# The second batch's products with x and with q in plain fp32, its q turned by TensorE, and the order written anew

## The chip, the core and the metric

The kernel runs on one core of one Trainium2 chip. A core has TensorE (PE, matrix products into PSUM), VectorE (DVE), ScalarE (ACT), GpSimd (POOL) and SyncE (SP, which here only issues DMAs). The metric is the device time of one execution in microseconds, given as the median of several runs. Each engine works through its own queue in order; a wait at the head of a queue holds everything behind it.

## The reference

The input x has 16 batches of 512 tokens with 256 features. Each batch goes through linear attention with 16 heads of 16 features, a residual and a layer norm, then a feed-forward layer with ternary weights, a residual and a layer norm:

```python
q, k, v = proj(Wq, bq), proj(Wk, bk), proj(Wv, bv)      # x @ W.T + b, per head
q_kern = exp(q - max(q));  k_kern = exp(k - max(k))      # max over the 16 features of a head
kv = einsum('bhsd,bhse->bhde', k_kern, v)
denom = einsum('bhqd,bhd->bhq', q_kern, sum_s(k_kern)) + 1e-06
y = einsum('bhqd,bhde->bhqe', q_kern, kv) / denom
x = layernorm(x + y @ Wo.T + bo)
Wq1, Wq2 = (clip(round(W / (mean(|W|) + 1e-5)), -1, 1) for W in (W1, W2))
x = layernorm(x + relu(x @ Wq1.T + b1) @ Wq2 + b2)
```

## The kernel before, in words

A batch is one tile of 128 partitions by 4 groups of tokens (t = 0 to 3) by 256 features. What TensorE does for a batch:

- `qk{t}` (L673 to L685): q and k of one group of tokens, 128x512, from xT and both weights. DVE adds the bias (`mxa`, L690) and takes the maximum (`mxb`, L696), POOL or DVE subtracts it (`mxs`, L700), ACT takes exp (`ex`, L711).
- `pks` (L758): the sum of exp(k) over all tokens, from a sum over the groups (`ks`, L734) that is split into two parts (`ksh`, `ksl`). DVE makes the denominators with it (`dena`, `denb`, `denc`), and `nrm{h}` (L790) divides exp(q) by them; the result is qs.
- `g{c}` (L813) or `gF{c}` (L809): the product of x with exp(k). The kernel uses that k_kern'v = (k_kern'x) Wv', so that v is never computed. `ge` (L832) copies the result, `kv` (L840) multiplies it with Wv, `kvm`, `kvp` mask it and add the bias' share, `m` (L868) multiplies with Wo.
- q turned: qs must have its features on the partitions.
- `o{h}` (L1066) or `oF{h}` (L1062): the product of the turned q with m. `or{t}` (L988) adds it to the residual, and the layer norm follows (`nm`, `nq`, `nv`, `np`, `na`: mean, squares, variance, pow on POOL, apply).
- x1 turned, then `f{f}` (L1098, 8 steps) and `z{f}` (L1135, 8 steps) for the feed-forward layer, with `ha`, `hc`, `hb` between them on ACT and DVE, and the second norm (`zr`, `ym` to `ya`), then the store.

Two ways to multiply are used. In plain fp32 one matmul takes the two fp32 operands. In the split way each operand is held as two rounded parts, high and low, and three products (high-high, high-low, low-high, `TERMS`) are summed. The split way needs the parts: a rounding copy on ACT and a subtraction on DVE or POOL for every operand: `xs`, `xsl0`, `xsl1` (L646, L652) for x, the second exp (L713) and `ek0`, `ek1` (L719) for exp(k), `me` and `ml` (L878, L883) for m, and `be`, `bl` (L928, L933) for the turned q.

Two ways to turn are used as well. TensorE turns 128x128 blocks against an identity (L941), and ACT copies the result out of PSUM; or a batch is "moved": DVE turns 32x32 blocks (`qtr`, L898), SP writes the tile to DRAM (`qtw`) and reads it back in four pieces that put the blocks in their places (`qtd`).

Constants say which batch does what: batches below FB, GB, OB take their products with the q/k weights, with x, and with q in plain fp32, and MOVED names the batches whose q (`qt`) and x1 (`xt1`) are moved:

```python
FB = 1
GB = 1
OB = 1
MOVED = {"qt": range(1, 16), "xt1": range(1, 15)}
        if b in MOVED[key]:
            moved()
            return
        for c in range(EC):
            one(c)
                if b < GB:
                    nc.tensor.matmul(s.pg[:, c, :], s.x32[:, t, cc], s.ex[:, t, E:2 * E],
                                     start=(t == 0), stop=(t == T - 1))
```

The order of all work is written out by hand: `ORDER` (from L109) gives each step of each batch a number, the steps are emitted by it, and each engine runs its instructions in the order in which they were emitted. `OTHER` (from L51) names the batches for which a step that two engines could do goes to the second of the two. Start-up steps stand in the same order: `lqk`, `wh`, `wl` load and split the q/k weights, `lw`, `sa`, `sr`, `tot`, `half`, `qn`, `qz` load the feed-forward weights and make them ternary, `warm` are matmuls without a use. The tile xt32 (the turned x from DRAM, `ldt0`, `ldt1`, L612) has two buffers, x32 (`ldx`, L640) has four. In PSUM, the `qk` products and all turns share two banks, `o`, `g`, `kv`, `m` and `pks` share two, `f` has two and `z` two.

Of the kernel before, what the change touches and what calls it, by code (L numbers as in the profile page):

```python
# [43 lines left out]
GB = 1  # L44
OB = 1
KB = 0
JB = 2
MOVED = {"qt": range(1, 16), "xt1": range(1, 15)}
# [3 lines left out]
    "xtl1": (1, 3, 7, 15),  # L52
    "qn2": (0,),
    "ks": (0, 1, 2, 4, 5, 8, 11),
    "ksl": (0, 1, 2, 3, 4, 5, 7, 8, 10, 11, 12, 13, 14, 15),
    "qn0": (0,),
    "xsl1": (1, 3, 12, 13),
    "qn1": (0,),
    "qn3": (0,),
    "mxs0": (1, 9, 10, 11, 12, 13, 14),  # L60
    "qn6": (0,),
    "nm0": (0, 1, 2, 3, 5, 7, 8, 9, 10, 11, 14),
    "ek0": (1, 3, 4, 8, 9, 10, 11, 12, 13, 14),
    "ek1": (1, 2, 3, 4, 6, 7, 8, 9, 11, 12, 13, 14, 15),
    "nv0": (0, 3, 8, 9, 13),
    "kvp": (1, 3, 4, 5, 7, 9, 12, 14, 15),
    "xb0": (1, 3, 7, 12, 15),
    "kvl": (1, 2, 3, 4, 5, 7, 8, 10, 11, 12, 13, 15),
    "xsl0": (2, 4),
    "xb1": (1, 3, 4, 13),  # L70
    "qn7": (0,),
    "qn4": (0,),
    "x1b1": (0, 6, 11),
    "qn5": (0,),
    "qtbl0": (2, 3, 4, 9, 15),
    "x1b0": (0, 1, 7, 9, 11, 12, 13),
    "xt1bl0": (1, 2, 3, 5, 7, 10, 14),
    "hc4": (1, 5, 6, 9, 14),
    "nrm0": (3, 7, 8, 9, 10, 11),
    "na0": (2, 6, 8, 14),  # L80
    "mxs1": (4, 7, 13, 14),
    "mxs2": (4, 7, 13, 14, 15),
    "xt1bl1": (2, 3, 4, 5, 6, 10, 12),
    "ym0": (1, 2, 5, 8),
    "na2": (3, 4, 15),
    "hc5": (2, 7, 13, 14, 15),
    "hc7": (2, 5, 10, 11, 12, 13, 15),
    "qtbl1": (4, 7, 15),
    "yv0": (2, 3, 4, 6, 11),
    "nrm1": (5, 11, 13, 14),  # L90
    "ya0": (2, 6, 7, 8, 12, 13, 15),
    "na1": (4, 7, 11, 14, 15),
    "mxs3": (7, 10, 13),
    "hc2": (4, 5, 6, 8, 11, 13, 14),
    "hc3": (4, 12, 13, 14),
    "ya3": (3, 6, 11, 12, 13),
    "hc6": (4, 8, 9),
    "xtl0": (10, 13),
    "hc1": (5, 7, 10, 11, 12, 15),
    "ya2": (4, 11, 13, 14, 15),  # L100
    "ya1": (5, 7, 11, 12, 13, 14),
    "hc0": (9, 10, 13, 14),
    "na3": (10, 13),
    "ym2": (15,),
    "yv1": (15,),
    "yv2": (15,),
    "ym3": (15,),
# [5 lines left out]
    "wh0": (3,),  # L113
    "ldt0a": (4, 0, 0, 0, 0, 0, 0, 0, 0, 0, 0, 0, 0, 0, 0, 0),
    "qkF0_0": (5, 0, 0, 0, 0, 0, 0, 0, 0, 0, 0, 0, 0, 0, 0, 0),
    "wl0": (6,),
    "ldt1a": (7, 0, 0, 0, 0, 0, 0, 0, 0, 0, 0, 0, 0, 0, 0, 0),
    "wh1": (8,),
    "wl1": (9,),
    "lbqk": (10,),  # L120
    "qkF0_1": (11, 0, 0, 0, 0, 0, 0, 0, 0, 0, 0, 0, 0, 0, 0, 0),
    "mxa0": (12, 101, 119, 271, 362, 547, 589, 741, 927, 1135, 1172, 1344, 1546, 1661, 1766, 1938),
    "ldt0": (0, 13, 61, 158, 231, 346, 335, 545, 743, 893, 792, 1025, 1049, 1380, 1562, 1505),
    "xt0": (0, 14, 62, 177, 257, 386, 387, 643, 809, 894, 831, 1113, 1220, 1402, 1644, 1808),
    "mxb0": (15, 113, 120, 279, 365, 550, 598, 744, 932, 1169, 1173, 1345, 1547, 1662, 1783, 1976),
    "ldt1": (0, 16, 72, 108, 208, 221, 411, 416, 690, 915, 826, 1099, 1082, 1363, 1631, 1725),
    "xt1": (0, 17, 77, 117, 239, 344, 467, 630, 775, 916, 901, 1231, 1218, 1392, 1657, 1847),
    "xtl1": (0, 18, 94, 141, 248, 402, 516, 634, 817, 933, 1024, 1249, 1219, 1393, 1705, 1848),
    "qkF1_0": (19, 0, 0, 0, 0, 0, 0, 0, 0, 0, 0, 0, 0, 0, 0, 0),
    "ldt1b": (20, 0, 0, 0, 0, 0, 0, 0, 0, 0, 0, 0, 0, 0, 0, 0),  # L130
    "mxs0": (21, 115, 155, 306, 420, 551, 662, 784, 961, 1170, 1326, 1401, 1548, 1672, 1826, 2008),
    "exF0": (22, 0, 0, 0, 0, 0, 0, 0, 0, 0, 0, 0, 0, 0, 0, 0),
    "ldt0b": (23, 0, 0, 0, 0, 0, 0, 0, 0, 0, 0, 0, 0, 0, 0, 0),
    "xtl0": (0, 24, 69, 183, 278, 413, 521, 659, 816, 945, 975, 1296, 1351, 1403, 1666, 1814),
    "qkF1_1": (25, 0, 0, 0, 0, 0, 0, 0, 0, 0, 0, 0, 0, 0, 0, 0),
    "mxa1": (26, 88, 160, 232, 322, 474, 670, 765, 871, 1053, 1184, 1394, 1452, 1680, 1840, 1903),
    "mxb1": (27, 89, 164, 244, 323, 514, 712, 799, 889, 1067, 1281, 1408, 1453, 1681, 1841, 1914),
    "lw0": (28,),
    "sa0": (29,),
    "mxs1": (30, 114, 165, 280, 446, 515, 730, 840, 953, 1100, 1300, 1409, 1511, 1728, 1842, 1990),  # L140
    "exF1": (31, 0, 0, 0, 0, 0, 0, 0, 0, 0, 0, 0, 0, 0, 0, 0),
    "lvo": (32,),
    "woh": (33,),
    "qkF2_0": (34, 0, 0, 0, 0, 0, 0, 0, 0, 0, 0, 0, 0, 0, 0, 0),
    "qkF2_1": (35, 0, 0, 0, 0, 0, 0, 0, 0, 0, 0, 0, 0, 0, 0, 0),
    "mxa2": (36, 58, 162, 205, 444, 472, 625, 783, 973, 1045, 1294, 1333, 1561, 1599, 1732, 1942),
    "mxb2": (37, 59, 185, 302, 447, 541, 626, 791, 974, 1107, 1305, 1334, 1563, 1605, 1733, 2004),
    "ldx": (38, 70, 179, 154, 326, 524, 642, 845, 931, 1076, 1269, 1386, 1556, 1706, 1717, 1948),
# [223 lines left out]
def block_kernel(ctx: ExitStack, tc: tile.TileContext, x, xT, wqT, wkT, wvT, woT,  # L372
# [221 lines left out]
    def steps(b):  # L594
# [632 lines left out]
```

## Time and profile before

| | us |
|---|---|
| median of 3 runs | 484.31 (484.08 to 484.88) |
| the profiled execution's own time | 484.78 |
| its span on the core | 483.1 |
| TensorE busy / share | 469.2 / 97% |
| DVE busy / share | 439.9 / 91% |
| ACT busy / share | 406.2 / 84% |
| POOL busy / share | 378.8 / 78% |
| first `f` of batch 0 starts | 47.93 |
| last matmul starts | 476.94 |

In a row of the trace the columns are the start, the length, the engine, the line and operation, the tile written and the tiles read, the size and a count; in square brackets stands the engine's idle time before it and who ended it. Matmuls are pipelined: a record of TensorE is longer than the distance to the next one, so the cost of a matmul is read from start to start. A plain fp32 matmul shows as two records. The granted TensorE clock was 0.999 of full speed over the span.

### The profile page before, as it was taken

The numbers are of one execution on the slowest core, as the hardware profiler recorded it, in microseconds if no ns is written. First come the engines' busy times: TensorE is split into PE (matmuls) and PEld (weight loads), VectorE is DVE, ScalarE is ACT, GpSimd is POOL, SyncE is SP. The second block draws the span as 40 slices with busy tenths as digits, with TensorE's granted clock in tenths as the row PEclk, the third lists the DMA queues.
The fourth block names the chain that finished last, engine by engine and source line by source line (L and its number), as shares of the span: only waits on it lengthen the run. The fifth ranks groups of instructions, "written<-read, shape, count | busy, mean of one in ns | idle before, by whom it ended". The sixth has DMA issues, their size and how long they took to land.

```text
span 483.1 us, 9025 instructions
## 1 busy us (share of the span) xinstructions
PE 469.2 (97%) x2976; PEld 415.9 (86%) x2976; DVE 439.9 (91%) x859; ACT 406.2 (84%) x923; POOL 378.8 (78%) x391
## 2 busy tenths in 40 slices
PE   8989999999999999999999999999999999999995
PEld 5567899899888998989989898889989898898984
DVE  2889999999999999999999998999999988998964
ACT  3897998998889788997987989688898979966774
POOL 1788898976958999896989799798898778744524
PEclk9999999999999999999999999999999999999999
DMA  6931325071542745345332605323445145124102
GB/s 227 309 140 43 89 88 196 24 229 55 160 125 68 216 143 153 104 127 175 130 133 87 199 22 188 118 99 121 152 130 148 51 156 150 44 89 132 44 1 88
DMA packets 36671, 59.84 MB, mean 124 GB/s; under 512 B 4240, under 2 KB 22672, under 8 KB 36624
## 3 DMA queue, kind: packets, MB, share of 16 engines
q1 hardware_dynamic: 36048, 58.74, 38.1%
q8 instruction: 23, 0.38, 0.3%
q10 hardware_dynamic: 576, 0.52, 0.3%
q14 instruction: 24, 0.20, 0.2%
HBM read 35.66 MB, written 23.59 MB: 123 GB/s over the span
## 4 chain that ended last, share of the span: by engine, by line
PE 79%; DVE 6%; POOL 5%; DMA 4%; ACT 3%; issue 2%; ACTq 0%; POOLq 0%; DVEq 0%
PE ph L1098 22%; PE pz L1135 21%; PE pqk L680 14%; PE po L1066 8%; PE pg L813 8%; PE pkv L840 2%; PE pm L868 2%; DMA w32qk<-in_wkT_dram 1%; DMA x<-in_x_dram 1%; POOL qk L700 1%; DMA w<-in_w1T_dram 1%; DVE x1b L1037 1%; PE pg L809 1%; PE pks L758 1%; POOL rstd_z L1020 1%
## 5 line engine op out<-in xcount | busy, mean ns | idle before, releaser
L1104 ACT ACTIVATE ph<-ph,b_sb 128x512 f32<-128x512 f32 x128 | 83.7, 657 | 20.9 <-PE ph L1098 19.9
L700 POOL TENSOR_TENSOR qk<-qk,mx 128x512 f32<-128x512 f32 x45 | 51.6, 1150 | 12.7 <-DVE mx L696 12.1
L690 DVE TENSOR_TENSOR qk<-pqk,bqk 128x512 f32<-128x512 f32 x64 | 43.2, 679 | 3.8 <-PE pqk L680 1.5
L696 DVE TENSOR_REDUCE mx<-qk 128x32 f32<-128x512 f32 x64 | 43.4, 679 | 1.2
L711 ACT ACTIVATE ex<-qk 128x512 f32<-128x512 f32 x64 | 40.4, 631 | 3.9 <-POOL qk L700 3.1
L790 POOL TENSOR_TENSOR qs<-ex,rden 128x512 f32<-128x512 f32 x22 | 26.2, 1204 | 13.2 <-DVE rden L782 13.1
L1005 ACT ACTIVATE junk_z<-x1b,nm_z 128x256 f32<-128x256 f32 x64 | 32.2, 505 | 2.4 <-POOL nm_z L999 2.2
L1035 ACT ACTIVATE x<-x,nmr_o,rstd_o 128x256 f32<-128x256 f32 x50 | 28.0, 600 | 7.3 <-POOL nmr_o L1022 7.3
L1005 ACT ACTIVATE junk_o<-x,nm_o 128x256 f32<-128x256 f32 x64 | 32.1, 503 | 0.4
L823 POOL TENSOR_TENSOR x<-x,bo_bc 128x512 f32<-128x512 f32 x23 | 30.6, 1335 | 0.1
L1081 POOL TENSOR_TENSOR x1b<-x,b_bc 128x512 f32<-128x512 f32 x22 | 29.5, 1346 | 1.4 <-ACT x L1035 1.4
L988 DVE SCALAR_TENSOR_TENSOR x1b<-pz,x1b 128x256 f32<-128x256 f32 x64 | 24.7, 417 | 1.7 <-PE pz L1135 1.5
L988 DVE SCALAR_TENSOR_TENSOR x<-po,x 128x256 f32<-128x256 f32 x64 | 24.3, 417 | 1.5 <-PE po L1066 1.0
L1035 ACT ACTIVATE x1b<-x1b,nmr_z,rstd_z 128x256 f32<-128x256 f32 x39 | 21.8, 598 | 4.2 <-POOL nmr_z L1022 4.2
L777 DVE TENSOR_REDUCE den<-dent 128x64 f32<-128x1088 f32 x16 | 20.5, 1281 | 0.2
L762 DVE TENSOR_TENSOR dent<-ex,pks 128x1024 f32<-128x1024 f32 x16 | 19.4, 1214 | 1.0 <-PE pks L758 1.0
L898 DVE STREAM_TRANSPOSE rqT<-qs 128x1024 f32<-128x1024 f32 x15 | 18.6, 1240 | 1.7 <-POOL qs L790 1.3
L1020 POOL TENSOR_TENSOR rstd_z<-var_z,expo 128x4 f32<-128x4 f32 (+1 forms) x19 | 19.2, 1011 | 1.0
L898 DVE STREAM_TRANSPOSE rx1T<-x 128x1024 f32<-128x1024 f32 x14 | 17.4, 1240 | 1.9 <-ACT x L1035 1.2
L1020 POOL TENSOR_TENSOR rstd_o<-var_o,expo 128x4 f32<-128x4 f32 x16 | 18.1, 1131 | 0.8
L840 PEld LDWEIGHTS pkv<-g,wv 128*128 128x128 f32 x128 | 16.2, 191 | 2.2 <-ACT g L832 1.3
L840 PE MATMUL pkv<-g,wv 128*128 128x128 f32 x128 | 17.0, 276 | 0.7 <-ACT g L832 0.7
(899 smaller groups left out, 2122.6 us busy)
## 6 DMA issues: line engine op xcount, KB each, us to landing
x<-in_x_dram SPq DMA_DIRECT2D x16, 512.0 KB, 4.5
xt<-in_xT_dram SPq DMA_DIRECT2D x30, 256.0 KB, 4.1
wqT<-rqT SPq DMA_DIRECT2D x15, 512.0 KB, 2.6
dqT<-wqT SPq DMA_DIRECT2D x60, 128.0 KB, 3.2
out_dram<-x1b SPq DMA_DIRECT2D x30, 256.0 KB, 2.2
wx1T<-rx1T SPq DMA_DIRECT2D x14, 512.0 KB, 2.6
dx1T<-wx1T SPq DMA_DIRECT2D x56, 128.0 KB, 3.2
w<-in_w1T_dram SPq DMA_DIRECT2D x4, 256.0 KB, 4.2
```

The lines of the kernel that those rows point to most:

```text
L680: nc.tensor.matmul(s.pqk[t], s.xt[i][:, c, tt], wqk[j][:, c, :], start=(c == 0 and n == 0), stop=(c == EC - 1 and n == 2))
L690: nc.vector.tensor_tensor(s.qk[t].rearrange("p g d -> p (g d)"), s.pqk[t], bqk, ALU.add)
L696: nc.vector.tensor_reduce(s.mx[t], s.qk[t], AX.X, ALU.max)
L700: engine(f"mxs{t}", b, nc.gpsimd, nc.vector).tensor_tensor(s.qk[t], s.qk[t], s.mx[t].unsqueeze(2).to_broadcast([P, 2 * NH, HD]), ALU.subtract)
L840: nc.tensor.matmul(s.pkv[:, cc], wv[:, ec, cc], s.g[:, ec, cc], start=(ec == 0), stop=(ec == EC - 1))
L988: nc.vector.scalar_tensor_tensor(out=r, in0=p[t], scalar=1.0, in1=r, op0=ALU.mult, op1=ALU.add, accum_out=stat("sum")[:, t:t + 1])
L1005: nc.scalar.activation(junk, getattr(s, what)[:, t, :], AF.Square, bias=n.nm[:, t:t + 1], accum_out=stat("sq")[:, t:t + 1])
L1020: nc.gpsimd.tensor_tensor(stat("rstd")[:, sl], n.var[:, sl], expo[:, sl], ALU.pow)
L1035: nc.scalar.activation(r, r, AF.Identity, bias=nmr, scale=rstd)
L1098: nc.tensor.matmul(s.ph[f], w1[:, c, f * P:(f + 1) * P], s.x1T[i][:, c, :], start=(n == 0), stop=(n == 2 * EC - 1))
L1104: nc.scalar.activation(s.ph[f], s.ph[f], AF.Relu, bias=b1_sb[:, f:f + 1])
L1135: nc.tensor.matmul(s.pz[t], hx[:, t * P:(t + 1) * P], w2[:, f, :], start=(done[tt] == 1 and t == tt[0] and i == 0), stop=(done[tt] == FC a ...
```

## The change

GB and OB go from 1 to 2, and batch 1 leaves `MOVED["qt"]`. So batch 1 takes its product with x from x and exp(k) as they are (8 fp32 matmuls in place of 24 split ones), its product with q likewise, and its q is turned by eight matmuls of TensorE and two copies of ACT. The steps that made the parts for it (`xs`, `xsl0`, `xsl1`, the second exp, `ek0`, `ek1`, `ml`, `qtr`, `qtw`, `qtd`, `be`, `bl`) go away for that batch. Batch 1's q and k are computed as before, from split operands. All of `ORDER` and of `OTHER` is written anew, for every batch; the functions stay as they are, three lines higher up.

The diff, cut to the constants and to rows of the tables for the first batches (the columns of a row of `ORDER` are the batches from 0 on; rows are cut after batch 4):

```diff
-GB = 1
-OB = 1
+GB = 2
+OB = 2
-MOVED = {"qt": range(1, 16), "xt1": range(1, 15)}
+MOVED = {"qt": range(2, 16), "xt1": range(1, 15)}
...
-    "nrm0": (3, 7, 8, 9, 10, 11),
+    "nrm0": (0, 5, 6, 7, 9, 11, 14, 15),
-    "nrm1": (5, 11, 13, 14),
+    "nrm1": (1, 2, 3, 8, 11),
...
-    "wh0": (3,),
-    "wh1": (8,),
+    "wh1": (3,),
+    "wh0": (7,),
...
-    "sa1": (90,),
+    "sa1": (78,),
-    "gF0": (60, 0, 0, 0, 0, ...),
+    "gF0": (65, 147, 0, 0, 0, ...),
-    "gF1": (80, 0, 0, 0, 0, ...),
+    "gF1": (75, 148, 0, 0, 0, ...),
-    "ge": (81, 169, 251, 405, 501, ...),
+    "ge": (84, 149, 261, 409, 528, ...),
-    "kv": (82, 181, 273, 415, 549, ...),
+    "kv": (89, 174, 289, 414, 529, ...),
-    "qt0": (99, 0, 0, 0, 0, ...),
+    "qt0": (100, 171, 0, 0, 0, ...),
-    "qteF0": (102, 0, 0, 0, 0, ...),
+    "qteF0": (102, 172, 0, 0, 0, ...),
-    "qt1": (104, 0, 0, 0, 0, ...),
+    "qt1": (112, 162, 0, 0, 0, ...),
-    "qteF1": (105, 0, 0, 0, 0, ...),
+    "qteF1": (113, 169, 0, 0, 0, ...),
-    "m": (111, 213, 298, 480, 649, ...),
+    "m": (103, 205, 316, 474, 612, ...),
-    "meF": (112, 0, 0, 0, 0, ...),
+    "meF": (108, 212, 0, 0, 0, ...),
-    "oF0": (125, 0, 0, 0, 0, ...),
+    "oF0": (119, 213, 0, 0, 0, ...),
-    "oF1": (131, 0, 0, 0, 0, ...),
+    "oF1": (120, 238, 0, 0, 0, ...),
-    "pks": (65, 148, 228, 383, 530, ...),
+    "pks": (66, 142, 226, 357, 509, ...),
-    "qk0": (0, 91, 118, 216, 283, ...),
+    "qk0": (0, 92, 116, 252, 322, ...),
-    "qk2": (0, 53, 161, 204, 366, ...),
+    "qk2": (0, 62, 132, 187, 415, ...),
-    "xt11": (170, 0, 0, 0, 0, ...),
+    "xt11": (166, 0, 0, 0, 0, ...),
-    "xt10": (174, 0, 0, 0, 0, ...),
+    "xt10": (178, 0, 0, 0, 0, ...),
-    "f0": (195, 398, 535, 704, 808, ...),
+    "f0": (184, 396, 542, 702, 827, ...),
-    "ldt0": (0, 13, 61, 158, 231, ...),
+    "ldt0": (0, 21, 51, 127, 211, ...),
-    "ldt1": (0, 16, 72, 108, 208, ...),
+    "ldt1": (0, 11, 60, 87, 217, ...),
-    "ldx": (38, 70, 179, 154, 326, ...),
+    "ldx": (45, 93, 128, 247, 384, ...),
```

In the order before, TensorE's steps around batch 1 are: gF0, warm1, pks, gF1, kv of batch 0; qk1, qk0 of 1; tot1; qt0, qt1, m of 0; qk0 of 2; oF0, oF1 of 0; pks of 1; qk1, qk2 of 2; g0, g1 of 1; xt11, xt10 of 0; kv of 1; qk3 of 2; f0, f3 of 0. In the new order they are: gF0, pks, gF1 of 0; qk1 of 1; warm1; kv of 0; qk0 of 1; tot1; qt0, m, qt1 of 0; qk0 of 2; oF0, oF1 of 0; qk2 of 2; pks, gF0, gF1 of 1; qk1 of 2; qt1 of 1; xt11 of 0; qt0, kv of 1; xt10 of 0; qk3 of 2; f0 of 0; qk2, qk1 of 3; f4 of 0; m of 1; z0 of 0; oF0 of 1; f3 of 0; pks of 2; oF1 of 1. On SP, ldt0 of batch 5 has the number 77 in the new order and ldt1 of batch 5 231, and their copies on ACT have 308 and 307. On ACT, meF of batch 1 comes after ex1, ex0, ex2, ex3 of batch 2 and ha0, ha4 of batch 0.

## The prediction

> **What bounds the kernel now.** I read first the busy times of the page, then the stretches by time, then TensorE's own waits, and last its timeline around the second batch.
>
> ```profile
> PE 469.2 (97%) x2976; PEld 415.9 (86%) x2976; DVE 439.9 (91%) x859; ACT 406.2 (84%) x923; POOL 378.8 (78%) x391
> ```
>
> TensorE is busy 97% of the span, and in the chain that ended last it holds 79%. An average hides where the missing 3% lie. The stretches show it (columns: stretch, its length, then PE, PEld, DVE, ACT and POOL busy, granted clock, DMA share, GB/s):
>
> ```profile
> 0.00:20.00 20.00, 16.68 (x56) 11.03 (x57) 10.65 (x23) 10.47 (x22) 7.37 (x15) 1.00 0.77 246
> 20.00:48.00 28.00, 25.43 (x141) 20.68 (x140) 25.98 (x50) 24.84 (x57) 23.97 (x21) 1.00 0.37 135
> 48.00:100.00 52.00, 52.00 (x331) 46.49 (x329) 49.77 (x93) 47.77 (x103) 46.56 (x44) 1.00 0.33 102
> 100.00:200.00 100.00, 99.01 (x648) 89.38 (x647) 95.04 (x184) 88.15 (x206) 83.16 (x84) 1.00 0.46 135
> 200.00:300.00 100.00, 100.00 (x636) 88.91 (x635) 95.40 (x182) 89.31 (x205) 90.28 (x86) 1.00 0.42 135
> 300.00:400.00 100.00, 99.13 (x660) 90.42 (x659) 94.59 (x183) 84.22 (x193) 84.61 (x88) 1.00 0.38 124
> ```
>
> From 48 us on TensorE has no holes but one of 1.0 and one of 0.9; before 48 it has 5.9. So work added to TensorE in the second batch costs its full price unless it falls into the opening's holes. What they wait for, from TensorE's waits (who, for whom, us, times, longest):
>
> ```profile
> PE pqk L670 <- DMA xt<-in_xT_dram: 1.3, 1, 1.3
> PE po L1066 <- DVE m_4l L883: 1.0, 1, 1.0
> PE pz L1135 <- DVE h_7l L1116: 0.9, 1, 0.9
> PE pg L809 <- DMA x<-in_x_dram: 0.7, 1, 0.7
> PE pqT L941 <- ACT qT L951: 0.7, 1, 0.7
> PE pkv L840 <- ACT g L832: 0.7, 1, 0.7
> PE pks L758 <- POOL ksd_1l L745: 0.4, 1, 0.4
> ```
>
> Five of the seven lie in the opening, three of them (pqT, pkv, pks) after 20 us, where order can fill them.
>
> **The change, part by part.** The durations are those of the profiled execution (span 483.1, its time 484.78, so 1.7 around the span; it is 0.47 above the median of 484.31). Differences are worked out on it and added to the median.
>
> ```profile
> 33.52 3.72 PE L1062 MATMUL po<-m,qT 128*128 128x256 f32 x16
> 57.87 2.87 PE pg L813 x24
> 60.73 2.88 PE po L1066 x24
> 44.20 1.24 PE L941 MATMUL px1T<-ident,x 128*128 128x128 f32 x8
> 45.27 1.06 PE L840 MATMUL pkv<-g,wv 128*128 128x128 f32 x8
> ```
>
> *Two products in plain fp32, on TensorE.* One takes 16 records instead of 24. From start to start a record takes (3.72-0.39)/15 = 0.222 us (0.39 being a lone record's length), so 16 take 3.55 against 2.88: +0.67 each, +1.34 for both. The trace's row says that fp32 costs 0.444 per matmul where one rounded term costs 0.12. The Trainium skill (FP8 and Floating Point Precision, TensorE Precision Notes) says that true fp32 makes four passes through the array. By four passes of 0.12 the two products would cost +1.92 instead, and the whole forecast 0.6 more; the row decides.
>
> *q turned by TensorE.* Eight records of 128x128; the eight of the first batch's x1 start at 44.20 and the next work at 45.27, so +1.07. The Trainium skill (TensorE: Matmul & The Clock Gate, Part 4) gives some 275 ns for a turn inside a kernel; eight would be 2.2, which speaks against this change by another 1.1, but here they follow each other at 0.13.
>
> TensorE in all: +1.34 + 1.07 = **+2.41 us**.
>
> *Off TensorE, in batch 1.* ACT loses the copy of xs (1.03), four exk (4 x 0.41) and two split copies of qT (2 x 0.62), and gains two whole ones (2 x 0.58): -2.75. DVE loses one xs remainder (0.63), the remainder of m (0.68) and the block transpose (1.25): -2.56. POOL loses one xs remainder (1.28), two exk (3.0) and two qT remainders (2.67): -6.95. SP loses a 512 KB write and four 128 KB reads, which took 2.6 and 3.2 us to land. All of this was covered by TensorE in the steady part and is worth nothing by itself; it counts through the opening, where DVE is busy 25.98 of 28.00.
>
> *Engines given anew.* Counted over both orders, POOL issues 15 fewer instructions and DVE 3. By the groups' means POOL loses some 10 us (mainly six xs and five turned remainders at 1.3 to 1.4 each, against five more max-subtracts at 1.15 and three more k-sum pairs at 2.2), DVE some 4.7 (seven casts of h at 0.68, five max-subtracts at 0.78, three k-sum pairs at 1.24, against six more applies, three more qs and eleven more remainders), ACT gains 0.3. Neither DVE nor POOL has the longest total, so nothing is booked, but there is a little more slack behind TensorE.
>
> *The opening's order, walked down with these durations.* The loads ahead of batch 0's x on SP are the same set, so x lands at 19.45 as before and the first product with x starts at 19.58. Ahead of that, wh1 stands before wh0, so both casts wait for the second half of the weights (8.97); with xtl1 of batch 1 also ahead on DVE the first eviction moves from 10.31 to about 11.45 and the last exp of batch 0 from 18.11 to about 18.65. Its cover is x's landing; without it this costs 0.5. On SP, ldt0 of batch 5 is issued early and holds one of the two xt32 buffers until step 309, so batches 3 and 4 share the other: ldt1 of 3 waits for POOL's xtl of batch 2 (about 24), and ldx of batches 1 and 2 queue behind it. They land about 29 and 30, needed at 34 to 37: no cost. On ACT sa1 stands ahead of ge, so the eviction of pg comes at about 24.5 instead of 23.99, and exp, kvh and the max-subtracts behind ACT's queue follow; TensorE has qk1 of batch 1 (1.40) and the warm matmuls there instead of waiting. Then m stands between the two turns (0.7 hole filled), and qk2 of batch 2 ahead of pks (0.4 filled). nrm0 of batch 0 is on DVE, 28.2 against 28.05 on POOL. I get: second turn done 30.05 (31.1 before), o of batch 0 from 31.45 (33.52), last residual add 36.1 (38.04), dena of batch 1 36.8 (38.73). Then the new path is the norm of batch 0, whose pow on POOL waits behind xsl0, xb0 and xtl1, and ACT's ge of batch 1 in front of the applies: x1 complete about 43.2. First f at about 47.0 against 47.93.
>
> By that point the new order has also done batch 1's turns and the dearer first product, 1.07 + 0.67 = 1.74. So it has recovered 0.93 + 1.74 = 2.67. Next late is o of batch 1: on ACT its meF stands behind three or four exp of batch 2 and ha4, about 53.5, and TensorE comes to it 0.3 to 0.8 earlier: +0.55. The chain of waits shows 0.02 to 0.14 at each hand-over between engines, which my walk leaves out; ten of them at 0.03: +0.3. Sum: 2.41 - 2.67 + 0.55 + 0.3 = **+0.6 us**. Recovery is bounded by nothing (0) and by the 2.57 of holes after 20 us plus a first f up to 1 us earlier still (about 3.5).
>
> *Batches 2 to 15 in a new order.* The trace can't show the new waits. Before has 1.0 + 0.9 + about 0.5 of small ones; the nearest row for a new one is again 1.0. Bounds: -2.4 (all gone) to +2.4 (twice as many); I take 0. In the tail the last tile is now an even one, which needs one more 0.2 on POOL, against 0.4 that the last add waited behind an apply: 0.
>
> Forecast: 484.31 + 0.6 = **484.9 us**.
>
> **Rivals.** *1, opening not recovered, slower.* DVE carries the opening, and one late link (the pow of batch 0's norm behind POOL's three steps, or ge behind sa1) makes first f no earlier than before: then only the 1.74 is recovered at best, or none. From a delay of 0.9 at first f on, it decides: 2.41 + 0.85 - 1.74 = +1.5 to +2.41 + 0.85 = +3.3; taken 486.6. For: TensorE's 97%, DVE's 93% in that stretch. Against: fewer instructions there on every other engine.
>
> *2, new waits in the steady part, slower.* One or two of the kind of the 1.0 before po: 484.9 + 1 to 2, taken 486.2. For: every queue is reordered, and a single xt32 buffer serves batches 3 and 4. Against: DVE and POOL have less to do.
>
> *3, faster.* The two waits at 142 and 309 go (1.9) and the opening is as walked: 484.9 - 1.9 = 483.0; with the holes of the opening gone too 482. For: DVE 4.7 and POOL 10 us lighter. Against: the load that decides is TensorE's, and it grows.
>
> **How the numbers follow.** This kernel can be told from no change at about 0.2%, 0.97 us. Chances: the forecast's case 0.32; rival 1 0.22; rival 2 0.18; rival 3 0.28. So faster 0.28, same 0.32, slower 0.40. The forecast's own range is 483.4 to 485.3; with the rivals, whose signs differ, 482.0 to 487.8.
>
> **What would show it.** Right: 16 records of about 3.55 for each product of batch 1 and eight turns at 0.13; TensorE busy about 471.6; first f before 47.5; a wait for m before o of batch 1; no waits for pkv and pqT near 24 and 30. Wrong: first f later than 48, a wait of over 1 us at TensorE between 50 and 460, or a POOL queue that TensorE waits for.

## The result: 1% slower, and the profile after

The changed kernel takes 489.38 us (489.02 to 489.91), the kernel before 484.60 beside it: a ratio of 1.0101, 95% interval 1.0083 to 1.0118. I had said 484.9, with 482.0 to 487.8 for the range.

The page's busy times, the kernel after:

```profile
PE 471.7 (97%) x2968; PEld 417.6 (86%) x2968; DVE 440.0 (90%) x856; ACT 406.1 (83%) x928; POOL 367.3 (75%) x376
```

TensorE is busy 97% here as well: the share says nothing of what happened. The stretches do (columns as in the prediction):

```profile
20.00:48.00 28.00, 27.09 (x146) 22.77 (x145) 26.65 (x52) 24.68 (x55) 20.42 (x19) 1.00 0.26 93
48.00:100.00 52.00, 50.39 (x301) 43.94 (x300) 48.47 (x90) 45.08 (x102) 42.48 (x40) 1.00 0.37 117
...
200.00:300.00 100.00, 98.37 (x630) 87.79 (x630) 95.97 (x187) 81.29 (x188) 82.56 (x81) 1.00 0.39 125
300.00:400.00 100.00, 98.41 (x652) 89.01 (x651) 93.00 (x178) 88.97 (x209) 84.02 (x83) 1.00 0.39 124
```

From 20 to 48 us TensorE has 0.9 of holes where it had 2.6; behind 48, in the three stretches shown, where it had none, none and 0.9, it has 1.6, 1.6 and 1.6. TensorE's own waits name them:

```profile
PE ph L1095 <- DVE h_1l L1113: 1.6, 2, 1.4
PE pqk L667 <- DMA xt<-in_xT_dram: 1.2, 1, 1.2
PE pkv L837 <- DVE x L985: 1.2, 1, 1.2
...
PE ph L1095 <- DVE h_0l L1113: 0.9, 1, 0.9
...
PE pks L755 <- POOL ksd_9l L742: 0.6, 1, 0.6
```

All of these but the second lie behind the opening, at 67.2, 348.6, 261.2 and 245.4. The two long waits that the order before had (po at 141, pz at 309) are gone.

The spans of the two profiles, cut at three events of TensorE. The first loads land at somewhat different times in different executions, so stages count from the first product with x:

| us | before | after | change | predicted |
|---|---|---|---|---|
| start of the first product with x | 19.58 | 19.71 | +0.13 | 0 |
| from there to the first `f` | 28.35 | 27.00 | **-1.35** | -0.93 |
| from there to the start of the last matmul | 429.01 | 434.08 | **+5.07** | +1.5 |
| from there to the end of the span | 6.13 | 6.73 | +0.60 | 0 |
| span | 483.07 | 487.53 | +4.46 | +0.6 |

The opening did better than forecast; the whole loss lies behind it. To see how much of the +5.07 is work and how much waiting, I take the distance from each matmul's start to the next and subtract the usual distance of its line (the median). With one median a line for both kernels, the usual distances add up to 461.4 before and 463.4 after, +2.0. The last matmul of a plain fp32 product is followed sooner than the usual distance, so read from the starts of the products and turns (below) the added work is **+1.6**. What exceeds the usual distance by over 0.02 is lost time:

| TensorE's lost time, us | 20 to 50 | 50 to 120 | 120 to 300 | 300 to end | all after 50 |
|---|---|---|---|---|---|
| before | 4.98 | 0.75 | 3.52 | 4.08 | 8.35 |
| after | 3.23 | 3.73 | 4.90 | 4.40 | 13.03 |

So +4.7 us of new waits behind the opening, 3.0 of it in the 70 us right behind it. (With the distances that fall short of the usual set against them, it is +4.5, and -2.7 in the opening; with the +2.0 of usual distances this makes up the 3.85 by which the last matmul starts later.)

### The profile page after: what moved, and what is told of

It reads as the page before. It is cut to its first block, busy times and chain, and to the rows that moved or that the text cites. A ratio compares the mean times of both kernels' runs of the same rounds, so it can differ in the third digit from the quotient of the medians.

```text
span 487.5 us, 9001 instructions
## 1 busy us (share of the span) xinstructions
PE 471.7 (97%) x2968; PEld 417.6 (86%) x2968; DVE 440.0 (90%) x856; ACT 406.1 (83%) x928; POOL 367.3 (75%) x376
## 5 line engine op out<-in xcount | busy, mean ns | idle before, releaser
L697 POOL TENSOR_TENSOR qk<-qk,mx 128x512 f32<-128x512 f32 x50 | 56.6, 1139 | 14.5 <-DVE mx L693 14.5
L820 POOL TENSOR_TENSOR x<-x,bo_bc 128x512 f32<-128x512 f32 x25 | 32.8, 1314 | 0.2
L1078 POOL TENSOR_TENSOR x1b<-x,b_bc 128x512 f32<-128x512 f32 x23 | 30.6, 1334 | 0.7 <-ACT x L1032 0.7
L1032 ACT ACTIVATE x<-x,nmr_o,rstd_o 128x256 f32<-128x256 f32 x45 | 25.0, 596 | 2.4 <-POOL nmr_o L1019 2.4
L787 POOL TENSOR_TENSOR qs<-ex,rden 128x512 f32<-128x512 f32 x19 | 21.5, 1137 | 5.5 <-DVE rden L779 4.7
L1017 POOL TENSOR_TENSOR rstd_z<-var_z,expo 128x4 f32<-128x4 f32 (+1 forms) x19 | 18.2, 962 | 7.0 <-ACT var_z L1011 6.2
L1032 ACT ACTIVATE x1b<-x1b,nmr_z,rstd_z 128x256 f32<-128x256 f32 x38 | 20.8, 595 | 0.8 <-POOL nmr_z L1019 0.7
L1017 POOL TENSOR_TENSOR rstd_o<-var_o,expo 128x4 f32<-128x4 f32 x16 | 16.8, 1050 | 3.9 <-ACT var_o L1011 3.2
L895 DVE STREAM_TRANSPOSE rqT<-qs 128x1024 f32<-128x1024 f32 x14 | 17.3, 1238 | 2.0 <-POOL qs L787 1.6
```

Source lines behind the costliest of these rows:

```text
L697: engine(f"mxs{t}", b, nc.gpsimd, nc.vector).tensor_tensor(s.qk[t], s.qk[t], s.mx[t].unsqueeze(2).to_broadcast([P, 2 * NH, HD]), ALU.subtract)
L1017: nc.gpsimd.tensor_tensor(stat("rstd")[:, sl], n.var[:, sl], expo[:, sl], ALU.pow)
L1032: nc.scalar.activation(r, r, AF.Identity, bias=nmr, scale=rstd)
```

## What the new waits have in common

DVE's instructions ahead of three of those waits, after (start, length, engine, line, operation, tiles):

```profile
66.38 1.83 DVE L577 SCALAR_TENSOR_TENSOR w<-w,half,neg 128x512 fp32r<-128x512 f32 x1
68.14 0.68 DVE L1113 TENSOR_TENSOR h_1l<-ph,h_1h 128x512 fp32r<-128x512 f32 x1
...
257.85 1.79 DVE L787 TENSOR_TENSOR qs<-ex,rden 128x512 f32<-128x512 f32 x1
...
347.56 1.78 DVE L1078 TENSOR_TENSOR x1b<-x,b_bc 128x512 f32<-128x512 f32 x1
```

and what POOL did at the time:

```profile
65.14 2.53 POOL L628 TENSOR_TENSOR xt_4l<-xt,xt_4h 128x512 fp32r<-128x512 f32 x2
...
257.81 1.28 POOL L820 TENSOR_TENSOR x<-x,bo_bc 128x512 f32<-128x512 f32 x1
...
347.45 1.35 POOL L716 TENSOR_TENSOR exk_13l<-ex,exk_13h 128x512 fp32r<-128x512 f32 x1 [1.73 <-ACT exk_13h L710]
```

Each of the three DVE instructions usually takes 0.68 to 0.74. Each began while POOL was at work, and each ended 0.54 to 0.55 us after POOL's instruction did: 68.21 after 67.67, 259.64 after 259.09, 349.34 after 348.80. It has no exception in these two traces: of the DVE operations on two tiles in SBUF, every one that took over 0.1 us longer than usual ran beside a POOL operation on a tile and ended 0.54 to 0.55 after it (0.28 to 0.29 where its own tile is half as wide), 29 before and 37 after. DVE's applies (one tile of 128x256 in SBUF) are held as well, 6 before and 9 after, and end 0.15 after POOL's instruction. DVE instructions that read PSUM (`h_1l` above, `mxa`, the residual adds) kept their length in all 254 and 243 cases in which they began beside a POOL operation on 128x512. The Trainium skill (SBUF — State Buffer, Who interferes with whom) says that a DVE instruction with two SBUF inputs contends with a GpSimd instruction that reads SBUF, and that the port pair which the two share is an exclusive lock. The traces agree; the 0.55 that follows is theirs.

So a DVE step that reads two SBUF tiles costs 0.68 or up to 1.8, by what POOL does at that moment, and what stands behind it on DVE is late by the difference. The profile of before shows it as well; the prediction left it out.

## The experiments

The stage lengths come from the profiled execution of each; the ratio is against the kernel before in the same set of runs. "f" is the first `f`; losses are TensorE's lost time as above.

| kernel | us | ratio, 95% | to f | f to last | lost 50-120 | 120-300 | 300- |
|---|---|---|---|---|---|---|---|
| before | 484.31 | | 28.35 | 429.01 | 0.75 | 3.52 | 4.08 |
| after | 489.38 | 1.0101 [1.0083, 1.0118] | 27.00 | 434.08 | 3.73 | 4.90 | 4.40 |
| 1 edit, old order | 488.58 | 1.0085 [1.0066, 1.0103] | 30.92 | 429.51 | 0.73 | 3.41 | 4.18 |
| 2 product with x alone | 486.27 | 1.0029 [1.0014, 1.0043] | 30.49 | 428.86 | 0.70 | 3.35 | 4.07 |
| 3 product with q and turn | 487.41 | 1.0060 [1.0044, 1.0075] | 30.32 | 429.30 | 0.69 | 3.12 | 4.19 |
| 4 edit, new opening, old rest | 486.28 | 1.0041 [1.0028, 1.0055] | 26.81 | 432.41 | 3.93 | 3.39 | 3.99 |
| 5 no edit, new later order | 492.28 | 1.0156 [1.0141, 1.0171] | 28.35 | 436.27 | 5.41 | 5.40 | 4.72 |
| 6 after, seven steps moved | 487.09 | 1.0052 [1.0032, 1.0073] | 26.74 | 433.27 | 4.24 | 5.08 | 2.96 |
| 7 after, two steps moved | 486.55 | 1.0049 [1.0031, 1.0067] | 27.02 | 432.71 | 3.51 | 5.33 | 2.95 |
| 8 and the division first | 488.10 | 1.0063 [1.0045, 1.0081] | 26.77 | 433.49 | 4.56 | 5.01 | 3.06 |
| 9 after, read-back first | 488.34 | 1.0070 [1.0058, 1.0082] | 26.78 | 433.36 | 2.73 | 5.18 | 4.39 |
| 10 8 and 9 together | 486.52 | 1.0038 [1.0025, 1.0051] | 27.01 | 431.71 | 2.63 | 5.09 | 2.95 |
| 11 before, three places | 483.76 | 0.9990 [0.9978, 1.0002] | 28.34 | 428.40 | 0.71 | 4.47 | 2.37 |
| 12 before, three, second try | 484.22 | 0.9999 [0.9986, 1.0012] | 28.42 | 428.24 | 0.76 | 4.26 | 2.38 |
| 13 12, opening changed | 488.63 | 1.0081 [1.0060, 1.0103] | 32.33 | 428.65 | 0.82 | 4.43 | 2.61 |
| 14 4, four places | 486.87 | 1.0045 [1.0029, 1.0062] | 26.81 | 433.50 | 5.50 | 4.32 | 2.66 |
| 15 before, two places | 483.04 | **0.9957** [0.9943, 0.9971] | 28.76 | 427.29 | 0.73 | 3.34 | 2.41 |
| 16 4, three places | 483.27 | **0.9967** [0.9952, 0.9981] | 26.90 | 429.51 | 2.67 | 3.29 | 2.41 |

In the short diffs below, `"qtr"[2]: 266` stands for the number of the step `qtr` of batch 2 in `ORDER`; a number with a fraction puts it between two others.

### Edit, opening and later order taken apart (1, 4, 5)

Run 1, the edit with every other step where it was (only `qt1`, `qt0` and then `kv` of batch 1 stand behind its product with x):

```diff
-GB = 1
-OB = 1
+GB = 2
+OB = 2
-MOVED = {"qt": range(1, 16), "xt1": range(1, 15)}
+MOVED = {"qt": range(2, 16), "xt1": range(1, 15)}
...
-    "kv": (82, 181, 273, 415, 549, ...),
+    "kv": (82, 169.6, 273, 415, 549, ...),
-    "qt1": (104, 0, 0, 0, 0, ...),
+    "qt1": (104, 168.2, 0, 0, 0, ...),
-    "qt0": (99, 0, 0, 0, 0, ...),
+    "qt0": (99, 168.4, 0, 0, 0, ...),
```

> The edit alone: batch 1 in plain fp32 with its q turned by TensorE, every other step at its old place (the two turns and kv of batch 1 stand right behind its product with x). Theory A (the loss of the changed kernel comes from waits of TensorE in the new order of the later batches, the edit only adds TensorE work): the added work, some 1.8 us by the distances between starts, is paid once because the old opening has nothing to swallow it: 486.0 to 487.0. Theory B (the edit itself carries the loss, through its turns in the shared PSUM banks and its dearer products): 488 to 490. Theory C (the edit is free and only the order matters): 484 to 485.

Run 4, the changed kernel up to step 240, all that is left in the order and on the engines of before (numbers counted through anew):

```diff
-    "f0": (184, 396, 542, 702, 827, ...),
+    "f0": (184, 389, 526, 695, 799, ...),
-    "kv": (89, 174, 289, 414, 529, ...),
+    "kv": (89, 174, 270, 406, 540, ...),
```

> The changed kernel up to its step 240 (the last residual add of batch 1, with the edit), then all remaining steps in the old order and on the old engines. Theory A: the new opening is ahead of the old one by 1.2 us at the first f with 1.5 us more work done, and the old later order has few waits: 483.3 to 484.8, level with the kernel before or better. Theory B (the edit carries the loss): 488 or more. Theory D (the new opening hands over a worse state, such as one buffer of the turned x for two batches): 487 or more, with waits of TensorE between 55 and 120 us.

Run 5, the kernel before up to step 300, without the edit, the rest in the new order and on its engines:

```diff
-    "f0": (195, 398, 535, 704, 808, ...),
+    "f0": (195, 405, 551, 711, 836, ...),
-    "kv": (82, 181, 273, 415, 549, ...),
+    "kv": (82, 181, 273, 423, 538, ...),
```

> The kernel before, without the edit, up to its step 300, then all remaining steps in the new order and on the new engines. Theory A: the waits of the new order come along without the edit: 487.5 to 490, TensorE's waits after 60 us sum up to 4 us or more. Theory B: 484 to 485.5.

Run 1 took 488.58, run 4 486.28, run 5 492.28. By its time run 1 stands in the range of theory B, but its loss lies elsewhere than the changed kernel's. In run 1 the later order is the old one, and behind the first `f` it costs 0.50, most of it the dearer product with q (0.4): lost time after 50 is 8.32 against 8.35. Nearly all of its price is in the opening, +2.57 to the first `f`. Run 4 took a time between the ranges of theories A and D. It has the fast opening (26.81) and, past 120 us, the losses of before to within 0.13, at the same places (po at 142.6, pz at 309.2). Run 5 has no edit at all and loses most: the waits of the changed kernel at 245, 261 and 349 come back at 248, 264 and 352. So the waits past 120 us belong to an order and come with it, with the edit or without. The losses between 50 and 120 in runs 4 and 5 have a part that only the joint of the two orders makes (1.97 at 66 in run 4, 3.8 in the 80s in run 5), so the two do not add up to the changed kernel.

TensorE's waits in run 5:

```profile
PE po L1063 <- ACT qT_2h L925: 1.3, 1, 1.3
PE pqk L667 <- DMA xt<-in_xT_dram: 1.3, 1, 1.3
PE pkv L837 <- DVE x L985: 1.2, 1, 1.2
...
PE ph L1095 <- DVE h_0l L1113: 0.9, 1, 0.9
```

### The two halves of the edit (2, 3)

```diff
-GB = 1
+GB = 2
```

> One half of the edit in the old order: only GB goes to 2, so batch 1's product with x is in plain fp32; its q goes by split parts and the block turn as before. TensorE +0.4 to +0.67. If the half brings no wait: 484.8 to 485.2. If the waits that the edit made in the old order (1.13 at 47.6, 0.46 more at 28, 0.48 more at 37) come with this half: 486 to 487.

```diff
-OB = 1
+OB = 2
-MOVED = {"qt": range(1, 16), "xt1": range(1, 15)}
+MOVED = {"qt": range(2, 16), "xt1": range(1, 15)}
```

> The other half in the old order: OB goes to 2 and batch 1's q is turned by TensorE. TensorE +0.67 + 1.07 = +1.74. With no wait: 486.0 to 486.4. If the new waits of the edit in the old order come with this half, which holds the two banks of the qk products for its two turns: 487.0 to 488.2.

The longer waits of run 1 at 28 and 37 (0.95 each, against 0.49 and 0.47 before) are in run 2 and not in run 3, so they come with the product with x. The wait of 1.13 ahead of qk of batch 2 at 47.4 is in run 3 and not in run 2, so it comes with the turns and with the place that runs 1 and 3 gave to `kv`. Run 3:

```profile
45.70 1.06 PE L840 MATMUL pkv<-g,wv 128*128 128x128 f32 x8
46.59 1.04 PE L941 MATMUL px1T<-ident,x 128*128 128x128 f32 x8
48.59 0.50 PE L680 MATMUL pqk<-wqkh,xt_2h 128*128 128x512 f32 x1 [0.96 <-DVE x1T_0l L964]
```

In the order before, `kv` of batch 1 stood between the turn of x1 and this `qk`, which needs the bank of that turn, and the loss there was 0.27; here it went ahead of the turn. So some 0.9 of the +2.57 may be the place of `kv` and not the edit; no run with these turns in the old opening has it elsewhere. In run 1 the wait stands as

```profile
PE pqk L680 <- DVE x1T_0l L964: 1.0, 1, 1.0
```

Run 2 took 1.6 more than the kernel before beside it (484.69), 0.9 to 1.2 above its work. Part of that is the granted clock, which was at half for some us in the profiled execution too; I come to it at the end.

### Can a wait be taken out of the new order? (6 to 10)

Run 6, seven steps at five places:

```diff
-"qtr"[2]: 266, "qz5": 268
+"qtr"[2]: 273.2, "qz5": 273.4
-"qtr"[9]: 1244, "x1b0"[10]: 1679, "xsl0"[9]: 1170
+"qtr"[9]: 1247.2, "x1b0"[10]: 1684.5, "xsl0"[9]: 1172.5
-"mxs1"[13]: 1659, "ex1"[13]: 1660
+"mxs1"[13]: 1663.5, "ex1"[13]: 1665.5
```

> The changed kernel with seven steps put later or earlier in its order (DVE: the turn of batch 2 and the ternary step qz5 behind hb1 of batch 0, the turn of batch 9 behind hb0 of batch 7, x1b0 of batch 10 behind the residual adds of batch 11, mxs1 of batch 13 behind ml of batch 11, with its ex1 on ACT; POOL: xsl0 of batch 9 behind ksl of batch 9). They stand ahead of what TensorE waits for at 67.2 (1.54 us), 348.6 (1.31), 261.2 (1.06), 245.4 (0.76) and 343.3 to 344.0 (0.83), 5.5 us in all. Theory L (these few waits are what the new order costs, each is local and worth its price): 484.0 to 485.6, the five waits gone. Rival S (DVE has no slack behind TensorE, so each wait comes back a few us later): 487 to 489.4.

Run 7, two of the seven:

```diff
-"qz5": 268, "x1b0"[10]: 1679
+"qz5": 273.4, "x1b0"[10]: 1684.5
```

> The changed kernel with only qz5 put behind hb1 of batch 0 and x1b0 of batch 10 behind the residual adds of batch 11. Both read two SBUF operands, and both took 1.1 us longer than usual in the profile of the changed kernel, ending 0.55 after the POOL instruction beside them. Theory K (a DVE instruction with two SBUF operands that starts beside a POOL instruction is held until it ends, and TensorE pays where something it needs stands behind): the waits at 67 and 348 shrink by about 1.1 each, 487.0 to 487.6, while DVE instructions with a PSUM operand put in their place keep their 0.4 and 0.68. Rival (the waits come from the links before, POOL's division for batch 2 and the banks of PSUM): both waits stay within 0.3, 488.8 to 489.4.

Run 6 gave 487.09, which the rival S expected; run 7 with fewer moves gave 486.55. From the first product with x to the last matmul, run 7 is 1.35 shorter than the changed kernel; the rest of the profiled execution's gain is a first product that started 1.4 earlier (18.28), which none of the moved steps stands ahead of. So that it came out below theory K's 487.0 to 487.6 is luck. DVE in run 7, at the two places:

```profile
64.98 0.65 DVE L1113 TENSOR_TENSOR h_1l<-ph,h_1h 128x512 fp32r<-128x512 f32 x1
65.55 1.27 DVE L577 SCALAR_TENSOR_TENSOR w<-w,half,neg 128x512 fp32r<-128x512 f32 x1
...
347.61 0.69 DVE L1078 TENSOR_TENSOR x1b<-x,b_bc 128x512 f32<-128x512 f32 x1
```

`h_1l`, with its PSUM operand, runs at full speed in the place where `w` was held, and `w`, still held, now holds nothing that TensorE needs; `x1b` is free. Both waits went, as theory K had it. But only one stayed away. Past 300 us the loss fell by 1.45 for good; between 50 and 120 it fell by 0.22, because TensorE, earlier by 1.1, then waited at 69 (0.59), at 82 (0.51) and in smaller pieces instead. Moving batch 2's turn back as well (run 6) made a new wait of 0.98 for `m_2l` at 79.

What holds TensorE there? In the changed kernel POOL does the division of batch 2's q (`nrm0`) behind the norm of batch 1, at 64.1, though its divisor was there at 61.3, and DVE's turn waits 1.1 for it. Run 8 puts that right:

```diff
-"nv0"[1]: 250, "np0"[1]: 251
+"nv0"[1]: 265.2, "np0"[1]: 265.4
```

> As the run with two steps put behind (qz5 and x1b0 of batch 10), and on POOL the variance and pow of batch 1's norm (nv0, np0) put behind nrm0 of batch 2. In the changed kernel that division starts at 64.1 though its divisor is there at 61.3; the turn of batch 2 on DVE waits 1.1 for it, and ACT 0.9 and DVE 1.0 for the turned q behind it. Theory C (this chain is the loss behind the opening): the turn starts near 62.7, both waits of DVE go, TensorE loses under 1.5 between 50 and 90 instead of 2.95, 484.8 to 485.6. Rival S (no slack, the loss comes back): 486.2 to 487, TensorE's loss between 50 and 120 stays near 3.5.

It gained nothing: 488.10, above what both theories gave, with 4.56 of loss between 50 and 120 against 3.51 in run 7. The turn on DVE did come 1.4 earlier, counted from the first product with x (63.06 against 65.21, that product at 18.98 against 19.71), but the read of the turned q went out only 0.4 earlier (70.60 against 71.69). SP's issues show why. The changed kernel:

```profile
66.49 0.33 SPq L902 DMA_DIRECT2D wqT<-rqT  x1
71.31 0.33 SPq L902 DMA_DIRECT2D wx1T<-rx1T  x1
71.69 2.27 SPq L909 DMA_DIRECT2D dqT<-wqT  x4
```

The read of batch 2's q (`dqT`) is queued behind the write of batch 1's x1 (`wx1T`), and that waits for DVE, as SP's waits say:

```profile
SPq L902 <- DVE rx1T L895: 4.4, 1, 4.4
```

In the order before, the read went out at 68.52, 2.4 after the write, and x1 was written after it. Run 9 moves that one step in the changed kernel; run 10 adds the moves of run 8:

```diff
-"qtd"[2]: 319
+"qtd"[2]: 282.5
```

> The changed kernel with one step moved: on SP the read of batch 2's turned q (qtd) ahead of the write of batch 1's x1 (xt1w), as in the order before. Theory Q (the read's place on SP's queue sets o of batch 2): the read is issued near 69.1 in place of 71.7, the wait of DVE for qT of batch 2 (1.0) goes, and TensorE's loss between 70 and 90 falls from 0.97 to 0.5 or less; the wait at 67 (1.54), which has another cause, stays. 488.4 to 489.0. Rival S: no change, 489.2 to 489.6.

> The changed kernel with the same move of qtd, and with nv0, np0 of batch 1 behind nrm0 of batch 2 on POOL, qz5 behind hb1 of batch 0 and x1b0 of batch 10 behind the residual adds of batch 11. With the division alone TensorE lost 3.35 between 60 and 90. Theory Q: the turned q is back near 70 to 71, ahead of o of batch 2, the wait of 0.82 at m_2l and that of 1.9 of DVE go, loss between 60 and 90 about 1.8 or less; from the first product with x to the last matmul 458.3 to 459.2 against 460.3. Rival S: 460 or more.

```profile
65.66 0.33 SPq L902 DMA_DIRECT2D wqT<-rqT  x1
68.28 1.75 SPq L909 DMA_DIRECT2D dqT<-wqT  x4
70.48 0.34 SPq L902 DMA_DIRECT2D wx1T<-rx1T  x1
```

In run 9 (whose first product with x starts at 19.09) the read goes out at 68.28 in place of 71.69, the four pieces take 1.75 to issue in place of 2.27, no loss is left between 70 and 90, and the time is 488.34, just below what theory Q gave. In run 10 the wait at 67 goes too (0.08 between 60 and 70, against 1.65 in the changed kernel), but one of 1.06 at 70.3 is new:

```profile
PE pz L1132 <- DVE h_2l L1113: 0.9, 1, 0.9
```

First product to last matmul is 458.72 against 461.08, in the range of Q. Between 50 and 120, though, run 10 lost 2.63, only 0.10 less than run 9: of the 1.1 gained there, 1.0 comes with the one step on SP. The division and the place of `w` gained nothing without it (run 8) and 0.1 with it; what else run 10 gained is `x1b`, as in run 7.

So some 2.4 of the 4.7 us have a cause that was shown by removing it: SP's queue behind the opening (1.0) and DVE's held `x1b` at 348 (1.45). That the held `w` delays `h_1l`, and with it TensorE at 67, was shown too, but the time came back as other waits. The waits at 245 and 261 could be moved but not removed in run 6 (0.76 and 1.06 there became 0.46 and 0.36, and from 120 to 300 it lost 5.08 against 4.90). Their causes are only argued: `ksl` of batch 9 behind a remainder of 1.3 on POOL, and `qs` held beside POOL.

### Can the waits be taken out of the old order? (11 to 13, 15)

Run 11, without the edit, the three longest later waits of before:

```diff
-"ks"[5]: 640, "m"[4]: 649, "me"[4]: 650, "ml"[4]: 651
+"ks"[5]: 651.5, "m"[4]: 647.3, "me"[4]: 647.5, "ml"[4]: 647.7
-"hb7"[8]: 1506
+"hb7"[8]: 1499.5
-"ya3"[11]: 2045
+"ya3"[11]: 2048.5
```

> The kernel before, nothing of the edit, with its three longest later waits worked on in the same way: ks of batch 5 behind ml of batch 4 and m, me, ml ahead of the last remainder of its turned q (wait of 1.15 at 141.3), hb7 of batch 8 ahead of dena of batch 11 (1.03 at 307.9), one apply of batch 11 behind hb4 of batch 12 (0.41 at 413.3). Theory L: 481.9 to 482.8, below the kernel before. Rival S: 484.0 to 484.6.

483.76, between the two ranges. Two of the three went for good (1.03 at 308 and 0.41 at 413). The third turned into a longer one, 1.56 at 142:

```profile
PE po L1066 <- ACT g L832: 1.4, 1, 1.4
```

`ks` of batch 5, put later on DVE, made `ksh` on ACT late, and ACT's `ge` behind `ksh` kept a bank of PSUM from `o`. Run 12 puts `ksh` behind `ge`:

```diff
-"ksh"[5]: 653, "ksl"[5]: 654
+"ksh"[5]: 660.5, "ksl"[5]: 660.7
```

> The kernel before with the same moves as in the run that mended three places, and ksh and ksl of batch 5 put behind ge of batch 5 on ACT and behind it on POOL. In that run two of the three waits were gone, and at the third ksh, held by the later ks, held ge and with it a bank of PSUM: 1.56 at 142.3 and 0.33 at 145.4 in place of 1.15. Theory L (each wait has one late link and goes with it): 481.8 to 482.7, no wait over 0.3 between 130 and 160. Rival S (the wait comes back once more): 483.3 to 484.4.

The wait came back a third time, 1.34 at 145, now in front of `pks`, which needs `ksl`. Three links hang on DVE's work in those 4 us, and it is full; here rival S was right. Run 15 leaves that place alone and keeps the two others:

```diff
-"hb7"[8]: 1506
+"hb7"[8]: 1499.5
-"ya3"[11]: 2045
+"ya3"[11]: 2048.5
```

> The kernel before with only two moves: hb7 of batch 8 ahead of dena of batch 11 (wait of 1.03 at 307.9) and one apply of batch 11 behind hb4 of batch 12 (0.41 at 413.3). Theory C, waits in the steady part are worth their price: 482.8 to 483.4. Rival S: 484.0 to 484.6.

483.04, and 0.9957, as theory C had it: from the first product with x to the last matmul it is 1.3 shorter than the kernel before, and two moved steps are worth what their waits showed, 1.4 (by the medians beside each other, 1.8). Run 13 tried three moves of TensorE's from the new opening, without the edit:

```diff
-"qk1"[1]: 87, "kvl"[0]: 110, "m"[0]: 111
+"qk1"[1]: 81.5, "kvl"[0]: 101.5, "m"[0]: 103.8
-"pks"[1]: 148, "dena"[1]: 149, ..., "kvb"[1]: 157
+"pks"[1]: 159.2, "dena"[1]: 159.4, ..., "kvb"[1]: 159.9
```

> As the run before it, and of the new opening only three moves of TensorE's, without the edit: qk1 of batch 1 ahead of kv of batch 0, m of batch 0 between its two turns (kvl with it), pks of batch 1 behind qk1 of batch 2 (with dena, denb, denc, nrm, kvb of batch 1). They fill the waits of 0.84 at 23.3, 0.84 at 29.2 and 0.47 + 0.62 at 36.5 to 37.2. If the opening is bound by TensorE's order, 1.5 to 2.2 less than that run: 480.0 to 481.0. If it is bound by the chain over DVE, ACT and POOL to the first x1, first f stays near 47.9 and the time within 0.6 of that run, or above it by the 1.1 to 1.4 by which dena comes later.

The first `f` came 4 us later, not earlier: with `kv` later, DVE's masks and `half` were late, and TensorE waited 2.21 for `half` at 27.5 and 1.43 for `kvd_0l` at 30.7. Some 1.7 of it is TensorE's clock, which was granted at 0.50 to 0.95 between 30 and 36 us here. The new opening is a set of moves on five queues; TensorE's part of it alone is worse than nothing.

### The edit with the better halves of both orders (14, 16)

Run 14 adds to run 4 the places of run 11 and a later `qtr` of batch 2:

```diff
-"qtr"[2]: 265
+"qtr"[2]: 272.5
```

> The edit with the new opening and the old later order, as in the run of the new opening alone (486.28), with the same three places mended and one more: the turn of batch 2 behind mxa0 of batch 3, hb1 of batch 0 and kvm, kvp of batch 2, which removes the wait of 1.97 at 66.2 at the joint of the two orders and most of the 0.44 at 72.4. Theory L: 486.3 - 2.4 - 2.6 = 481.3, taken 481.0 to 482.5, so as fast as or faster than the mended kernel before, though it carries the 2.4 us of added TensorE work. Rival S: 485 to 486.3.

486.87, no gain, and above both ranges: the wait at the joint came back as 0.89, 0.71 and 0.82 between 67 and 75, and the one at 145 was that of run 11. DVE in run 4 had waited 2.8 us for ACT's `h_5h` ahead of the joint, with the denominators of batch 2 behind it. Run 16 moves that step instead, and keeps the two places that had held:

```diff
-"hb5"[0]: 248
+"hb5"[0]: 253.5
-"hb7"[8]: 1497, "ya3"[11]: 2036
+"hb7"[8]: 1490.5, "ya3"[11]: 2039.5
```

> The edit with the new opening and the old later order, as in the run of the new opening alone (486.28), with three moves: hb5 of batch 0 behind denb and denc of batch 2 on DVE, where DVE waited 2.8 for it, POOL's division 5.0 behind that, and TensorE 1.97 at 66.2; hb7 of batch 8 ahead of dena of batch 11; one apply of batch 11 behind hb4 of batch 12. Theory C: TensorE's loss between 50 and 80 falls from 3.5 to about 1, and 1.4 more go after 300: 482.0 to 483.3, below the kernel before with 2.4 us more of work on TensorE. Rival S: 484.6 to 486.2.

483.27, 0.9967, at the upper end of theory C: three moved steps take 3.0 off run 4. TensorE's waits in run 16:

```profile
PE pqk L670 <- DMA w32qk<-in_wkT_dram: 1.4, 1, 1.4
PE pwarm L466 <- DVE eps L435: 1.1, 1, 1.1
PE po L1066 <- DVE m_4l L883: 1.0, 1, 1.0
PE tot L554 <- DVE half L549: 0.6, 1, 0.6
PE ph L1098 <- DVE x1T_1l L933: 0.5, 1, 0.5
```

The only one of 1 us behind the opening is the old one at 141. Runs 15 and 16 both beat the kernel before and the changed one, and can't be told from each other: between these two orders the edit is worth nothing either way. What it costs TensorE, 1.6, its opening gives back (-1.45 to the first `f`, with most of that work already done). Whether a still better order exists for either was not tried.

## Why the prediction was wrong, step by step

- **TensorE's work: +2.41 forecast, +1.6 found.** Both products were mis-sized. The changed kernel:

```profile
31.64 3.62 PE L1059 MATMUL po<-m,qT 128*128 128x256 f32 x16
36.71 3.62 PE L806 MATMUL pg<-ex,x 128*128 128x256 f32 x16
...
41.92 0.66 PE L938 MATMUL pqT<-ident,qs 128*128 128x128 f32 x4 [0.18 <-POOL qs L787]
```

 The product with x goes from 36.71 to the next matmul at 39.98, 3.27 against 2.87 split: +0.40, not +0.67. I had counted the last record at the full distance, but what follows it starts 0.03 after, and the distance of my row (0.222) held a wait; it is 0.216. The product with q takes 3.27 against 2.87 in runs 1 and 3, +0.4 too; in the changed kernel it comes in two halves of 1.64 and 1.54, +0.3. The turns are 8 of 0.11, 0.9 and not 1.07. The estimate of +0.6 from the four passes of the Trainium skill (FP8 and Floating Point Precision, TensorE Precision Notes) stands further off still: a plain fp32 matmul took 2 x 0.216 = 0.43 here against 0.12 for a split term, 3.6 times.
- **The opening: right, and better.** Second turn at 29.75 to 30.16 (30.05 forecast for its end), `oF` of batch 0 at 31.64 (31.45), the last residual add about 36.4 (36.1), the denominators of batch 1 at 36.95 (36.8), first `f` at 46.71 (47.0). Rival 1 is out. Run 1 shows what the new opening is for: in the old one the edit as placed there costs 2.57 to the first `f`. The prediction's list of waits lacked `warm` (1.1, at the start) and `tot` (0.6 in the opening); both stand in the changed kernel as well.
- **The wait for m before `oF` of batch 1: +0.55 forecast, 0.23 found** (at 52.9).
- **"Batches 2 to 15 in a new order ... I take 0": this is the step that failed.** It was +4.7 of lost time, outside its bounds of ±2.4. I bounded it by the waits that the old order had, as if they were a sample of what an order has. Runs 4 and 5 show that each order brings its own waits, and past 120 us brings them whole; the old one was low in them, 0.75 in the 70 us behind the opening, and that is a property of its order, not of the work. My rival 2 named the mechanism, but with "one or two of the kind of the 1.0", 486.2: it was four of 0.8 to 1.5, a pair of 0.45 and 0.38 at 343 to 344, and several of up to 0.34. The single buffer of xt32, which I gave as its reason, shows in none of the waits.
- **"Neither DVE nor POOL has the longest total, so nothing is booked, but there is a little more slack": the slack is not there.** The new table of engines gives DVE eleven more remainders and three more divisions, most of them with both operands in SBUF. The 37 held instructions lost 15.9 us by it, the 29 of before 10.5 (each against its usual 0.69, 0.74 or 0.42), and the held applies 4.4 against 3.6. Held time counts as busy, and so the page shows DVE at 440.0 against 439.9 where I had counted 4.7 us less: the longer holds, 6.2, are more than that.
- **SP's queue.** I walked SP for the loads of x and missed that the read of batch 2's q stands behind the write of batch 1's x1. Run 9 prices it: 0.94 from the first product to the last matmul.
- **The tail: 0 forecast, +0.60.** No run was made for it, but the profiles place it: it is 6.1 in the old later order without batch 1's q turned by TensorE, 6.3 with it, and 6.5 to 6.8 in every kernel with the new later order.

The sign I had named for it is there: "a wait of over 1 us at TensorE between 50 and 460" stands twice among the waits, and a third just below it.

## What to carry to other kernels

In a kernel whose order is fitted by hand to within a few per cent of its busiest engine, a new order is a change in itself, and not one of size 0: price it by walking each queue through the stretch behind the edit, with every read-back behind a write, every SBUF-only step of DVE beside a step of POOL, and every step behind which the busiest engine's next operand stands. Where a wait is to be removed, ask first whether the link behind it is on time, and put steps that read PSUM, which POOL held in none of some 500 cases here, ahead of those that read SBUF twice. And before you reorder everything for an edit, look for the two or three longest waits that are there already: two moved steps gained as much here as any reordering did.

## What the hardware showed that I had not expected

The hold of DVE by POOL is exact: 0.54 to 0.55 us from the end of POOL's instruction to the end of DVE's for tiles of 128x512, whatever remained of POOL's when DVE's began, in all 56 such cases of the two profiles. POOL's `pow` on 128x4, which takes 1.03 us, held none: `qs` at 40.10 beside one took 0.69.

TensorE's granted clock was halved for some 3.4 us in the middle of the opening in some executions. The stretches of run 2:

```profile
28.00:30.00 2.00, 1.22 (x9) 0.73 (x7) 1.97 (x5) 1.97 (x4) 1.09 (x2) 1.00 0.05 17
30.00:32.00 2.00, 1.32 (x8) 1.16 (x7) 1.97 (x6) 1.80 (x5) 2.00 (x2) 0.75 0.41 132
32.00:34.00 2.00, 2.00 (x9) 1.80 (x8) 1.06 (x2) 1.91 (x5) 2.00 (x2) 0.50 0.00 0
34.00:36.00 2.00, 2.00 (x9) 1.66 (x9) 0.69 (x1) 1.32 (x3) 1.48 (x2) 0.90 0.00 0
```

TensorE waits 1.5 of the 4 us from 28 to 32, and from 31 to 34.5 it has half its clock; matmuls start 0.43 apart instead of 0.23. It happens in some executions and not in others: those of run 2 with a mean clock of 0.993 took 486.6 to 487.1, those of 0.997 to 0.999 took 485.2 to 486.0. Run 12 shows the same (0.993 and 0.994: 485.3 to 485.9; 0.996 to 0.999: 483.8 to 484.3). The holes alone don't bring it about: in the profiled execution of run 1 TensorE waits as long between 28 and 32, and the clock stays at 1.00. Nor does the new opening, with fewer holes, keep it away for certain: of run 4's five executions two had a mean clock of 0.993 and 0.992 and took 487.0 and 487.4, the other three (0.996 to 0.999) 485.8 to 486.3. In the eight of run 16, with the same opening, the mean never fell below 0.996, and they lie within 482.9 to 484.1. What sets it off stays open.
